# A twelve-stage network on one Trainium2 core: the decay chain of two state-space mixers cut into pieces, and a shared expert in three blocks

## The chip, the cores and the metric

The kernel is one program on one core of a Trainium2 chip. The core has engines that each run their own queue of instructions in order: TensorE (PE; loading weights is listed apart as PEld), VectorE (DVE), ScalarE (ACT), GpSimd (POOL) and SyncE (SP), which here only issues DMAs. They wait for one another through semaphores. The metric is the time of one execution on the device in microseconds (us), lower is better. Three executions of the kernel before took 2148.16, 2151.61 and 2161.24 us; the median is 2151.61 us.

## The reference

The network works on 1024 tokens in two sequences of 512, with 256 features in fp32. It has four layers, each of the form ffn, attention or mixer, ffn, and each part is added to the running `x`. The stages that the change touches are these:

```python
# layer 0, ffn (used twice): 32 experts, 6 per token, and one shared expert of width 352
x = x + 0.5 * _L0_ffn_ref(_layernorm(x, axis=-1), L0_ffn_wg_router, ...)
    sh = jax.nn.silu(x2d @ ws_gate) * (x2d @ ws_up) @ ws_down
    return y + sh
# layers 2 and 3, mixer: a gated state-space layer, 8 heads in layer 2, 64 in layer 3
    zxbcdt = u @ W_in                                  # u is the layer norm of x
    dt = jax.nn.softplus(dt + dt_bias)
    xBC = sum((xp[:, w:w + L, :] * conv_w[:, w] for w in range(D_CONV))) + conv_b
    xBC = jax.nn.silu(xBC)                             # split into x, B, C
    y, final_state = ssd(x * dt[..., None], A * dt, Bm, Cm, CHUNK)
    y = y + x * D_param[:, None]
    yf = y * jax.nn.silu(z)
    rrms = jax.lax.rsqrt(jnp.mean(yf * yf, axis=-1, keepdims=True) + 1e-05)
    y = yf * rrms * norm_w
    return y @ W_out
```

`dt` is a positive step size per token and head, `A * dt` its log decay (dA), and `ssd` sums over earlier tokens with weights exp(cumulative decay), within a chunk by a masked product and from chunk to chunk by a state.

## The kernel before

`x` stays in SBUF as 8 chunks of 128 tokens; a sequence of 512 tokens, 4 chunks, is called a row, 0 or 1 (the code's `b`). The stages run one after the other. Most of their order is chosen by a scheduler when the program is built; where `in_order` (L134) is used, the order in which the code is written is fixed on the engines named.

**Layer 0's shared expert.** `load_shared` (L266) loads gate, up and down weights and cuts the width of 352 into four blocks of 88. `shared_unit` (L280) does one row: for each block `front` (pg and pu at L291, silu at L294, product h at L295), and one block later `back`, which adds into `acc` (L301); at the end two adds into `x` (L319). Both rows run while `slot_lists` (L334) works out on DVE and PE in which slot each token of each expert goes (`sl_oh` L382, `ps_sl` L399, `ps_slt` L419, `sl_put` L428, `sl_get` L429). With `sl_get`, POOL starts to gather tokens (`xe`, L453); the experts then run on PE as units of `ps_xe` (transposes, L467), `ps_gu` (L477), `ps_he` (L491), `ps_ye` (L502), and POOL puts results back (`rows`, L507). The results are read back by `add_rows` (L621 to L628), which is put off until the next stage calls `settle` (L155).

**The mixers** (`mamba`, L1381 to L1806). One unit is a row and a group of 8 heads, one step is a chunk of 128 tokens of a unit. Layer 2 has one group, so 2 units and 8 steps; layer 3 has 8 groups, 16 units and 64 steps. Before the first step stands a prelude:

- `row(b)`: layer norm (DVE L181, L182, L193; POOL for the reciprocal root, L189 and L190), then 8 transposes (L169) into `xT`, half of it copied by DVE (L126), half by ACT (L128).
- `decay_sums(b)`: `pd` on PE (L1434), then a chain over DVE and ACT (softplus with Exp L1442 and Ln L1444, L1437 to L1451) to dA, then on PE `ps_row` (L1457), `ps_cum` (L1475) and two `ps_dec` (L1479). The cumulative rows `cr` go to DRAM (L1468, two DMAs for each group of heads) and come back broadcast to all partitions as `lm` and `ce` (L1581, L1584).
- `conv`: a projection `pp` (L1487), a scaled copy `cacc` on ACT (L1491), three taps on DVE (L1493), silu on ACT (L1496). It is used for B, C and the four pieces of x of a unit (`prep_front`, L1554); `prep_back` transposes a finished piece (`pt` L1567, copy `xt` L1568).
- `products` (L1515 to L1522): C times B. `exponents` (DVE, 8 instructions, L1594), `raised` (ACT exp, L1599) and `masked` (L1603) make the decay weights of two chunks.

In a step, PE computes the gate's input `pz` (L1618), the output `py` (L1646), the projection of the step before (L1691) and the new state `pst` (L1661); DVE adds to `y` (L1672) and POOL multiplies the gate in (L1673). A step also prepares one piece of the next unit. The steps are written in order for PE, ACT, DVE and POOL; the prelude isn't: the scheduler places it. Its program order is row 0's norm, `decay_sums(0)`, the convs of B and C and of unit 0, exponents and raised, then `row(1)` and `decay_sums(1)`, and then the steps. PSUM tiles of `psM` rotate through three buffers.

Of the kernel before, what the change touches and what calls it, by code (L numbers as in the profile page):

```python
# [79 lines left out]
class Net:  # L80
# [116 lines left out]
    def layernorm_T(self, es, psum):  # L197


        xT = es.enter_context(self.tc.tile_pool(name="xT", bufs=1)).tile([P, KD, T], F32, name="xT")  # L200
        p = es.enter_context(self.tc.tile_pool(name="ln", bufs=1))

        def row(b):
            xn = p.tile([P, CB, D], F32, tag="xn", name="xn")
            self.layernorm(p, xn, b)
            self.transpose_tokens(xn, xT, psum, b)

        return xT, row
# [57 lines left out]
    def load_shared(self, g, up, down, f, bw=88):  # L266
        nc = self.nc
        w = self.w("wsh")
        gv = w[:, : KD * f].rearrange("p (k f) -> p k f", k=KD)
        uv = w[:, KD * f : 2 * KD * f].rearrange("p (k f) -> p k f", k=KD)  # L270
        dv = w[:bw, 2 * KD * f : 2 * KD * f + f // bw * D].rearrange("p (c d) -> p c d", d=D)
        nc.sync.dma_start(gv, g.rearrange("(k p) f -> p k f", p=P))
        nc.sync.dma_start(uv, up.rearrange("(k p) f -> p k f", p=P))
        nc.sync.dma_start(dv, down.rearrange("(c p) d -> p c d", p=bw))
        return [
            (gv[:, :, i * bw : (i + 1) * bw], uv[:, :, i * bw : (i + 1) * bw], dv[:, i, :], bw)
            for i in range(f // bw)
        ]
# [728 lines left out]
    def l1_ffn(self):  # L1007
        nc, tc = self.nc, self.tc
        with ExitStack() as es:
            psM = es.enter_context(tc.tile_pool(name="f1m", bufs=8, space=PSUM))  # L1010
            xT, row = self.layernorm_T(es, psM)
# [286 lines left out]
    def l2_ffn(self):  # L1298
        nc, tc = self.nc, self.tc
        E = 8  # L1300
        with ExitStack() as es:
            psM = es.enter_context(tc.tile_pool(name="f2m", bufs=8, space=PSUM))
            xT, row = self.layernorm_T(es, psM)
# [77 lines left out]
    def mamba(self, pre, win, wout, nh):  # L1381
# [11 lines left out]
        TOP = 85.0  # L1393
        wname, win, wout = win, a[pre + win], a[pre + wout]
        with ExitStack() as es:
            psM = es.enter_context(tc.tile_pool(name=pre + "m", bufs=3, space=PSUM))
            xT, row = self.layernorm_T(es, psM)
# [22 lines left out]
            rows = dram.tile([2, NG, NC, HG * P], F32, name="rows")  # L1420
            wk = es.enter_context(tc.tile_pool(name=pre + "w", bufs=2))

            def decay_sums(b):
# [18 lines left out]
                nc.scalar.activation(t1, t2, AF.Exp)  # L1442
                nc.vector.tensor_scalar(t2, t1, 1.0, None, ALU.add)
                nc.scalar.activation(da, t2, AF.Ln)  # L1444
                nc.vector.scalar_tensor_tensor(t2, t2, -1.0, t1, ALU.add, ALU.subtract)
# [10 lines left out]
                for cc in range(CB):  # L1456
# [6 lines left out]
                    )  # L1463
                nc.vector.tensor_copy(cr[:, 0, :], ps)
                nc.scalar.activation(cr[:, 1, :], ps, AF.Exp)
                for g in range(NG):
                    for i in range(2):
                        nc.sync.dma_start(  # L1468
                            rows[i, g, bs].rearrange("c (h t) -> h c t", t=P),
                            cr[g * HG : (g + 1) * HG, i, :].rearrange("h (c t) -> h c t", t=P),  # L1470
                        )
# [4 lines left out]
                nc.vector.tensor_tensor(jb[:, bs, :], jb[:, bs, :], ps, ALU.subtract)  # L1476
                for out, lhsT in ((dec, self.c["gt"]), (cd, self.ones)):
# [5 lines left out]
            def conv(wv, m, b, out):  # L1483

                pp = psM.tile([P, S], F32, tag="mm", name="pp")
# [4 lines left out]
                acc = wk.tile([P, S], F32, tag="cacc", name="cacc")  # L1490
                nc.scalar.mul(acc, pp, cw[:, m, 3:4])  # L1491
                for w in range(2, -1, -1):
                    nc.vector.scalar_tensor_tensor(  # L1493
                        acc[:, 3 - w :], pp[:, : S - 3 + w], cw[:, m, w : w + 1], acc[:, 3 - w :], ALU.mult, ALU.add
                    )
                return lambda: nc.scalar.activation(out, acc, AF.Silu, bias=cb[:, m : m + 1])  # L1496
# [5 lines left out]
            def conv_b(b):  # L1502
                BTs[b] = wk.tile([P, S], F32, tag="BT", name="BT", bufs=1)
                conv(wb[:, :, 0:P], NX, b, BTs[b])()

            def conv_c(b):
                conv(wb[:, :, P : 2 * P], NX + 1, b, CT[:, b * S : (b + 1) * S])()
# [46 lines left out]
            def prep_front(u, m):  # L1554
                wo, g = u["wo"], u["g"]
                silu = conv(u["wx"][:, :, m * P : (m + 1) * P], g * NM + m, u["b"], u["xc"][:, m, :])
# [5 lines left out]
                return rest  # L1562
# [10 lines left out]
            def fetch(u, cc):  # L1573
# [7 lines left out]
                nc.sync.dma_start(k["lm"].rearrange("p h t -> p (h t)"), rows[0, u["g"], c].partition_broadcast(P))  # L1581
                if cc > 0:
                    k["ce"] = wk.tile([P, HG, P], F32, tag="ce", name="ce", bufs=3)
                    nc.sync.dma_start(  # L1584
                        k["ce"].rearrange("p h t -> p (h t)"), rows[1, u["g"], c].partition_broadcast(P)
# [150 lines left out]

            row(0)
            decay_sums(0)
            conv_b(0)
            conv_c(0)  # L1740
            for i in range(min(2, len(order))):
                fetch_wx(*order[i])
            unit(0)
            for i in range(3):
                chunk(i)
            products(0)
            for m in range(NM):
                prep_front(us[0], m)()
                if m:
                    prep_back(us[0], m - 1)  # L1750
            for i in (0, 1):
                exponents(ks[i])
            raised(ks[0])
            back = (us[0], NM - 1)
            row(1)
            decay_sums(1)


            tail = {}
            for s in range(NS):  # L1760
# [4 lines left out]
                with self.in_order(tail):  # L1765
# [9 lines left out]
                    rest = prep_front(unit(n + 1), cc) if nxt else None  # L1775
# [22 lines left out]
                with self.in_order(tail):  # L1798
                    new_state(k)

                    if last and cc == 0:
                        conv_b(1)
                    elif last and cc == 1:
                        conv_c(1)
                    elif last and cc == CB - 1:
                        products(1)  # L1806
            squares(ks[NS - 1])
# [66 lines left out]
```

## Time and profile before

| | us |
|---|---|
| median of three executions | 2151.61 |
| the profiled execution's own time | 2080.09 |
| its span, first to last instruction | 2078.0 |
| PE busy in it | 1786.1 |
| DVE, ACT, POOL busy | 1150.1, 791.6, 872.2 |
| layer 0's first ffn: first `pg` to first expert transpose `ps_xe` | 34.16 to 88.12 |
| the same in its second call, `ps_xe` | 518.72 |
| layer 2's mixer: first transpose to first `py` | 978.37 to 1036.69 |
| layer 3's mixer: first transpose to first `py` | 1324.76 to 1396.15 |

All lines of the profile come from one execution, so durations are compared with that execution's 2080.09 us. A timeline line gives start and duration in us, the engine, the line of code, the operation, output<-inputs, sizes and the number of instructions in the group; in brackets stands how long the engine was idle before it and what ended that. SPq is a DMA issue on SP. The granted clock is the share of TensorE's full clock that the chip allowed; over the whole span it was 0.912.

### The profile page before, as it was taken

How to read it: one execution, taken by the hardware profiler on the slowest of the kernel's cores; microseconds unless marked ns; L12 is line 12 of the kernel's file. 1: busy time of each engine (PE TensorE's matmuls, PEld its weight loads, DVE VectorE, ACT ScalarE, POOL GpSimd, SP SyncE). 2: the span in 40 equal slices, each digit the busy share in tenths (PEclk: the TensorE clock that was granted, in tenths of full speed). 3: DMA queues.
4: the chain of work that ended last, by engine and by line, in shares of the span. 5: the costliest groups of instructions: out<-in, count | busy, mean ns of one | idle time of the engine just before them, and what ended most of it. 6: DMA issues, size and time to landing. Idle time of an engine off the chain costs nothing. (4 is left out here: it accounts for less than half of the span.)

```text
span 2078.0 us, 29564 instructions
## 1 busy us (share of the span) xinstructions
PE 1786.1 (86%) x10590; PEld 1283.9 (62%) x10590; DVE 1150.1 (55%) x2725; ACT 791.6 (38%) x1336; POOL 872.2 (42%) x808
## 2 busy tenths in 40 slices
PE   5999859889999369889697989469999999999895
PEld 3677636565777247654476457347777677777664
DVE  4433266126333566556563653368777767777443
ACT  1132224210223024310562012357777667777211
POOL 3377646302777101000042026115666546676353
PEclk9999979989999669989797989679999999999798
DMA  8266450141565600000230013324444435444132
GB/s 294 62 194 187 144 187 2 31 143 34 177 183 154 221 0 1 21 1 0 93 103 21 11 36 98 106 98 153 155 153 159 153 121 174 153 163 134 42 94 94
DMA packets 117590, 226.03 MB, mean 109 GB/s; under 512 B 22532, under 2 KB 68978, under 8 KB 117292
## 3 DMA queue, kind: packets, MB, share of 16 engines
q1 hardware_dynamic: 88284, 170.17, 24.8%
q0 software_dynamic: 20608, 48.45, 7.3%
q10 hardware_dynamic: 8528, 5.26, 0.8%
q8 instruction: 93, 1.52, 0.3%
q14 instruction: 77, 0.63, 0.1%
HBM read 195.13 MB, written 41.81 MB: 114 GB/s over the span
## 5 line engine op out<-in xcount | busy, mean ns | idle before, releaser
L453 POOL DMA_INDIRECT xe<-table,sl_get x176 | 179.9, 1022 | 210.3 <-DVE sl_get L429 150.7
L477 PE MATMUL ps_gu<-we,xeT 128*128 128x352 f32 x704 | 228.3, 465 | 0.0
L507 POOL DMA_INDIRECT rows<-ye,sl_put x176 | 177.1, 1006 | 88.3 <-issue 41.4
L1493 DVE SCALAR_TENSOR_TENSOR cacc<-pp,L_attn_cols,cacc 128x511 f32<-128x511 f32 (+2 forms) x240 | 179.1, 748 | 55.5 <-ACT cacc L1491 50.2
L189 POOL TENSOR_SCALAR ln_rstd<-ln_mv 128x4 f32<-128x4 f32 x22 | 5.1, 233 | 420.1 <-DVE ln_mv L182 418.7
L502 PE MATMUL ps_ye<-we,hT 88*128 88x256 f32 x704 | 168.3, 379 | 2.9 <-ACT ye L128 1.6
L482 DVE SCALAR_TENSOR_TENSOR he<-se,xe,ps_gu 128x176 f32<-128x176 f32 x176 | 70.0, 398 | 174.3 <-ACT se L481 165.1
L477 PEld LDWEIGHTS ps_gu<-we,xeT 128*128 128x128 f32 x704 | 127.7, 193 | 54.7 <-issue 2.5
L502 PEld LDWEIGHTS ps_ye<-we,hT 88*128 88x128 f32 x704 | 133.0, 190 | 37.0 <-ACT ye L128 3.6
L1594 DVE SCALAR_TENSOR_TENSOR lm<-lm,jb,top 128x128 f32<-128x128 f32 x576 | 154.4, 343 | 0.0
L1618 PE MATMUL pz<-xT,wt 128*128 128x128 f32 x1152 | 143.1, 278 | 9.7 <-DVE cacc L1493 5.6
L1691 PE MATMUL yacc<-wt,y 128*128 128x256 f32 x576 | 145.8, 396 | 0.7 <-POOL y L1673 0.7
L1618 PEld LDWEIGHTS pz<-xT,wt 128*128 128x128 f32 x1152 | 136.2, 194 | 14.6 <-issue 9.2
L1487 PE MATMUL pp<-xT,wx 128*128 128x512 f32 x288 | 143.2, 623 | 0.3 <-ACT cd L1480 0.3
L1673 POOL TENSOR_TENSOR y<-y,sg 128x512 f32<-128x512 f32 x72 | 91.5, 1271 | 103.4 <-DVE y L1672 95.3
L1611 POOL TENSOR_TENSOR ce<-ce,CT 128x1024 f32<-128x1024 f32 x54 | 127.9, 2369 | 0.0
L169 PE MATMUL ps_tr<-cst,xn 128*128 128x128 f32 x176 | 42.5, 401 | 94.3 <-DVE xn L193 83.5
L1691 PEld LDWEIGHTS yacc<-wt,y 128*128 128x128 f32 x576 | 104.9, 192 | 25.4 <-issue 12.0
L1333 PE MATMUL ps_y<-w8T,xT 128*128 128x512 f32 x256 | 117.8, 614 | 0.0
L1646 PE MATMUL py<-lm,xt 128*64 128x128 f32 x1152 | 109.1, 284 | 5.9 <-issue 5.4
L481 ACT ACTIVATE se<-ps_gu 128x176 f32<-128x176 f32 x176 | 55.9, 318 | 149.8 <-PE ps_gu L477 149.7
L1603 DVE TENSOR_TENSOR lm<-lm,M 128x1024 f32<-128x1024 f32 x72 | 87.2, 1215 | 41.8 <-ACT lm L1599 40.3
(373 smaller groups left out, 3540.4 us busy)
## 6 DMA issues: line engine op xcount, KB each, us to landing
lm<-rows SPq DMA_DIRECT2D x72, 512.0 KB
ce<-rows SPq DMA_DIRECT2D x54, 512.0 KB
rows<-zero POOLq DMA_DIRECT2D x16, 768.0 KB, 10.0
y<-rows SPq DMA_DIRECT2D x16, 768.0 KB
we<-in_L_ffn_w_gate_dram SPq DMA_DIRECT2D x64, 176.0 KB
we<-in_L_ffn_w_up_dram SPq DMA_DIRECT2D x64, 176.0 KB
we<-in_L_ffn_w_down_dram SPq DMA_DIRECT2D x64, 176.0 KB
we<-in_L_ffn_w_dram SPq DMA_DIRECT2D x48, 176.0 KB
```

What stands on the lines that cost most here:

```text
L453: nc.gpsimd.indirect_dma_start(xe[:, i, :], None, table, bass.IndirectOffsetOnAxis(get[:, e * per + j : e * per + j + 1], 0), bounds_check ...
L477: nc.tensor.matmul(pg, xeT[:, k, i * P : (i + 1) * P], wgu[:, :, k], start=(k == 0), stop=(k == KD - 1))
L502: nc.tensor.matmul(py[:, i, :], hT[:, q, i * P : (i + 1) * P], wd[:, q, :], start=(q == 0), stop=(q == 1))
L507: put_rows = nc.gpsimd.indirect_dma_start(rows, bass.IndirectOffsetOnAxis(put[:, e * per + j : e * per + j + 1], 0), y[:, i, :], None, bou ...
L1333: nc.tensor.matmul(ps, xT[:, k, cs], self.w8T[:, k, 2 * e2 : 2 * e2 + 2, :], start=(k == 0), stop=(k == KD - 1))
L1487: nc.tensor.matmul(pp, wv[:, k, :], xT[:, k, b * S : (b + 1) * S], start=(k == 0), stop=(k == KD - 1))
L1493: nc.vector.scalar_tensor_tensor(acc[:, 3 - w :], pp[:, : S - 3 + w], cw[:, m, w : w + 1], acc[:, 3 - w :], ALU.mult, ALU.add)
L1594: nc.vector.scalar_tensor_tensor(k["lm"][:, h, :], k["lm"][:, h, :], jb[:, k["c"], n : n + 1], top, ALU.add, ALU.min)
L1611: nc.gpsimd.tensor_tensor(k["ce"], k["ce"], ct, ALU.mult)
L1618: nc.tensor.matmul(pz[:, m, :], u["wz"][:, kk, m * P : (m + 1) * P], xT[:, kk, c * P : (c + 1) * P], start=(kk == 0), stop=(kk == KD - 1),)
L1646: nc.tensor.matmul(py[i * HP : (i + 1) * HP, m, :], w[:, h * HP : (h + 1) * HP], v[:, h, :], start=(m == 0 and n == 0), stop=(n == len(src ...
L1691: nc.tensor.matmul(yacc[cc // 2][:, cc % 2, :], k["y"][:, m, :], u["wo"][:, m, :], start=(u["g"] == 0 and m == 0 and cc % 2 == 0), stop=(u ...
```

## The change

Three things are changed. First, the shared expert's blocks are as wide as the 128 partitions where more than two are needed: 352 is cut into 128, 128 and 96, and the down weights come in two DMAs. A width of 176 stays at two blocks of 88.

Second, `decay_sums` becomes a generator that stops at four places (behind the Exp, behind the Ln, behind `ps_row`, behind `ps_cum`), so that its pieces can be placed between other work, and `conv` returns its taps and its silu apart. `row` is split into `norm` and `turn`. The whole prelude stands in one order written out by hand for PE, ACT and DVE. In layer 2 (`few`), row 1's norm and turn follow row 0's first piece, and its decay chain is placed among the convs of unit 0. In layer 3, row 1's results of the expert stage are added to `x` ahead of C's taps (`settle(1)`), and its norm, turn and chain are hung on steps 0 to 4 (`later`), at the end of each.

Third, the DRAM layout of the rows has no group index any more, so that two DMAs per row of tokens write it, in place of two per group. The buffers of `cacc` are three in layer 3.

```diff
-    def load_shared(self, g, up, down, f, bw=88):
+    def load_shared(self, g, up, down, f):
+        n = -(-f // P)
+        bw = P if n > 2 else f // n
...
-        nc.sync.dma_start(dv, down.rearrange("(c p) d -> p c d", p=bw))
+        full = f // bw
+        nc.sync.dma_start(dv[:bw, :full], down[: full * bw].rearrange("(c p) d -> p c d", p=bw))
+        if full < n:
+            nc.sync.dma_start(dv[: f - full * bw, full], down[full * bw :])
...
-            rows = dram.tile([2, NG, NC, HG * P], F32, name="rows")
+            rows = dram.tile([2, NC, nh * P], F32, name="rows")
...
                 nc.scalar.activation(t1, t2, AF.Exp)
+                yield
                 nc.vector.tensor_scalar(t2, t1, 1.0, None, ALU.add)
                 nc.scalar.activation(da, t2, AF.Ln)
+                yield
...
+                yield
                 nc.vector.tensor_copy(cr[:, 0, :], ps)
                 nc.scalar.activation(cr[:, 1, :], ps, AF.Exp)
-                for g in range(NG):
-                    for i in range(2):
...
+                for i in range(2):
+                    nc.sync.dma_start(
+                        rows[i, bs].rearrange("c (h t) -> h c t", t=P),
+                        cr[:, i, :].rearrange("h (c t) -> h c t", t=P),
+                    )
...
                 nc.vector.tensor_tensor(jb[:, bs, :], jb[:, bs, :], ps, ALU.subtract)
+                yield
...
-                acc = wk.tile([P, S], F32, tag="cacc", name="cacc")
+                acc = wk.tile([P, S], F32, tag="cacc", name="cacc", bufs=2 if few else 3)
...
-            row(0)
-            decay_sums(0)
-            conv_b(0)
-            conv_c(0)
...
-            row(1)
-            decay_sums(1)
+            later = {}
             tail = {}
+            with self.in_order(tail, ("PE", "Activation", "DVE")):
+                row(0)
+                fetch_wx(*order[0])
+                d0, d1 = decay_sums(0), decay_sums(1)
+                next(d0)
+                if few:
+                    row(1)
+                bt, bs_ = conv_b(0)
+                bt()
+                next(d0)
+                ct, cs_ = conv_c(0)
+                self.settle(1)
+                ct()
+                next(d0)
+                if few:
+                    bs_()
+                    cs_()
+                unit(0)
+                fetch_wx(*order[1])
+                pf = [prep_front(us[0], 0)]
+                pf[0][0]()
+                next(d0)
+                next(d0, None)
+                if few:
+                    next(d1)
+                    next(d1)
+                else:
+                    bs_()
+                    cs_()
+                for i in range(3):
+                    chunk(i)
+                pf.append(prep_front(us[0], 1))
+                products(0)
+                pf[1][0]()
+                pf[0][1]()
+                pf[1][1]()
+                prep_back(us[0], 0)
+                pf.append(prep_front(us[0], 2))
+                pf[2][0]()
+                pf[2][1]()
+                prep_back(us[0], 1)
+                if few:
+                    next(d1)
+                    next(d1)
+                    next(d1, None)
+                exponents(ks[0])
+                exponents(ks[1])
+                pf.append(prep_front(us[0], 3))
+                pf[3][0]()
+                pf[3][1]()
+                raised(ks[0])
+                prep_back(us[0], 2)
+                back = (us[0], NM - 1)
+                if not few:
+                    later[0] = [lambda: norm(1)]
+                    later[1] = [lambda: turn(1), lambda: next(d1)]
+                    later[2] = [lambda: next(d1), lambda: next(d1)]
+                    later[3] = [lambda: next(d1)]
+                    later[4] = [lambda: next(d1, None)]
...
                     new_state(k)
...
+                    both(later.get(s, ()))
```

## Prediction, made before the result was known

> **What bounds the kernel now.** I read the page's head and busy shares first, then busy time by stage, then the order of time on TensorE (PE) at the three places that the diff touches.
>
> ```profile
> span 2078.0 us, 29564 instructions
> PE 1786.1 (86%) x10590; PEld 1283.9 (62%) x10590; DVE 1150.1 (55%) x2725; ACT 791.6 (38%) x1336; POOL 872.2 (42%) x808
> ```
>
> PE is busy for 86%, so an edit pays where it shortens PE's work or opens one of PE's gaps. By stage (window; its length; busy us and instructions of PE, weight load, DVE, ACT, POOL; granted TensorE clock; DMA share; GB/s):
>
> ```profile
> 34.00:74.00 40.00, 37.42 (x378) 20.88 (x378) 31.54 (x121) 5.30 (x8) 1.78 (x4) 1.00 0.24 78
> 74.00:88.00 14.00, 13.11 (x45) 7.65 (x43) 3.52 (x7) 1.19 (x2) 10.49 (x11) 1.00 0.28 77
> 978.00:1000.00 22.00, 13.07 (x51) 7.93 (x52) 11.03 (x34) 9.21 (x16) 1.26 (x2) 0.77 0.40 136
> 1000.00:1020.00 20.00, 13.59 (x42) 7.19 (x42) 13.52 (x25) 13.25 (x18) 0.00 (x0) 0.83 0.24 89
> 1020.00:1036.00 16.00, 11.37 (x53) 7.63 (x53) 3.72 (x14) 8.35 (x15) 0.21 (x1) 0.68 0.01 2
> 1376.00:1396.00 20.00, 14.57 (x61) 11.58 (x60) 7.00 (x16) 7.71 (x13) 0.72 (x1) 0.58 0.06 14
> 1396.00:1440.00 44.00, 44.00 (x334) 33.56 (x334) 35.32 (x79) 34.45 (x49) 27.66 (x20) 1.00 0.40 134
> ```
>
> Layer 0's shared expert (34 to 88) fills PE at full clock. The preludes of layer 2's mixer (978 to 1037) and layer 3's (1325 to 1396) leave PE idle for a quarter to two fifths, at a clock of 0.58 to 0.83: chains set their length, not work. Layer 3's steps (from 1396) leave PE no gap at all, with DVE and ACT at 80%.
>
> **Part 1, the shared expert in 3 blocks.** The hand-over to the experts, PE and POOL:
>
> ```profile
> 64.76 4.37 PE L399 MATMUL ps_sl<-sl_ol,sl_oh 128*32 128x64 f32 x224 [1.90 <-DVE sl_oh L382]
> 83.49 3.62 PE L301 MATMUL acc<-wsh,h 88*128 88x256 f32 x16
> 88.12 0.71 PE L467 MATMUL ps_xe<-cst,xe 128*128 128x128 f32 x4 [1.01 <-DMA xe<-table,sl_get]
> ...
> 74.47 1.11 POOL L453 DMA_INDIRECT xe<-table,sl_get  x1 [36.84 <-DVE sl_get L429]
> 75.88 1.03 POOL L453 DMA_INDIRECT xe<-table,sl_get  x1 [0.30 <-issue]
> ```
>
> A block of one half costs 4 matmuls for pg, 4 for pu and 8 for acc: three groups of 1.72 us (PE starts them at 78.33, 80.06, 81.77 and 83.49), 5.16 us. The matmuls' row count doesn't change with a block of 128 in place of 88. One block less, two halves, two calls: 4 x 5.16 = 20.6 us of PE work leave. Not all of it is time. The routing chain on DVE (sl_oh, until PE's 64.76) isn't shortened, and the same PE work lies ahead of it in both orders. So the saving falls behind it: PE, at 70.5 when ps_sl ends, has three acc groups left (5.2 us, and the turn of the slot table), not two fronts and five acc groups, and is through at about 77. Then the gathers set the start. They come at 1.30 us each from 74.47; elsewhere (gather at 1237.32 for 1.16, its ps_xe at 1240.54) a gather is used 2.1 us after its end. The first ps_gu needs two units, four gathers: 78.52 + 1.00 + 2.1 + 0.6 for ps_xe = 82.2. It stood at 90.22: **-8.0**. In the second call the fourth gather (509.21) comes some 0.7 later, behind one x add of L319: 513.6 for 520.82, **-7.2**. Bounds: -9 each if gathers land sooner, -4 each if POOL takes it back. The second load of `down` and the smaller ACT and DVE count lie under PE's work: nothing. Sum -15.2 (-8 to -18).
>
> **Part 2, layer 2's prelude.** Now, PE in order of time:
>
> ```profile
> 1026.67 1.87 PE L1457 MATMUL ps_row<-cst,dA 128*8 128x128 f32 x8 [3.40 <-DVE dt L1451]
> 1030.73 3.78 PE L1487 MATMUL pp<-xT,wx 128*128 128x512 f32 x4 [0.29 <-ACT cd L1480]
> 1036.69 1.09 PE L1646 MATMUL py<-lm,xt 128*64 128x128 f32 x16
> 1038.68 1.88 PE L1487 MATMUL pp<-xT,wb 128*128 128x512 f32 x4
> ```
>
> Row 1's chain stands alone from 1020.5 to 1030.7: 10.2 us that the change opens. What it adds is a fixed order on PE, ACT and DVE, in place of the scheduler's, which today runs exponents on DVE at 998 to 1004 while it waits. I add up along the new order. Row 1's norm (4 x 0.41, 1.47 waiting for POOL's rstd, 1.4) and turn end at 989.4; before, conv B started at 989.50, so it costs nothing yet. Conv B at half clock 3.2, its cacc 0.69, taps 2.3 (1015.32: six in 4.54): 995.6. Conv C's taps end at 999.1, and only behind them stand row 0's four dA instructions, so ps_row is at 1000.0 (it was at 985.43). Conv x0 stands behind ps_row on PE: its taps run 1006.1 to 1008.4 (now 1005.23). Behind them: cr, jb, ps_dec, row 1's pd (2.0), its Exp, Ln and two table loads of 1.28, the products; x1's taps end at about 1018 to 1020 (13.4 now). ACT then runs both silus and pt's copies ahead of x2's cacc: x2's taps end at 1026.5 to 1028 (about 1017.6). Row 1's dA, ps_row (1.9), cr: 1032. Both exponents, 16 x 0.27 = 4.3: 1036.7. x3's taps 2.3, silu with its load 2.0, raised with its load 3.2, 1043; masked 1.2, pz and py: 1047.1. It was 1036.69: **+10.4**, and the steps behind keep their order. The opened 10.2 us is overspent because exponents, taps and silus, which ran beside the convs, are now one behind the other.
>
> The size hangs on TensorE's clock. The row first: pp x4 takes 3.78 us at 1030.73 and 1.88 at 1038.68. The Trainium skill (TensorE: Matmul & The Clock Gate, Part 1: The HAM clock gate) has half rate after an idle window of about 3.4 us, and full rate only after as much sustained work. My chain leaves PE no 3.4 us of work at a stretch, so by the rule nearly every record on it runs cold: +10 to +12. By the rows of this prelude (granted 0.68 to 0.83) it would be warm for half of the time: about +7. All warm, seven groups at 1 us or so less: +3; all cold with an unlucky phase: +13. I take +10.4: the convs, pd and ps_row on the path are those that follow a gap.
>
> **Part 3, layer 3.** Now:
>
> ```profile
> 1375.40 2.19 PE L169 MATMUL ps_tr<-cst,xn 128*128 128x128 f32 x8 [9.67 <-DVE xn L193]
> 1377.73 3.78 PE L1434 MATMUL pd<-wb,xT 128*128 128x64 f32 x16
> 1386.80 1.94 PE L1457 MATMUL ps_row<-cst,dA 128*64 128x128 f32 x8 [5.28 <-DVE dA L1448]
> 1391.39 2.61 PE L1487 MATMUL pp<-xT,wx 128*128 128x512 f32 x4
> 1396.15 1.09 PE L1646 MATMUL py<-lm,xt 128*64 128x128 f32 x16
> ```
>
> From the x adds at 1367.97 to 1391.4, 23 us, row 1 is on the path of the first py. Moved to the steps, it leaves. The same sum along the new order: x adds (8, 2.8 us) now ahead of C's taps, dA to 1342, ps_row and x0's conv to 1346, cr 1350, B and C's silus 1353 to 1355, x1's taps to 1360, x2's 1367, exponents to 1371, x3's taps 1373, raised 1377, py 1381: **-15** (-12 to -16 with the clock's phase). The sixteen row DMAs (5.74 us of issue on SP) become two; nothing waits for them: exponents came 16 us after cr and come 16 us after it again. Row 1's four y loads (2.1 us of issue on SP) move from 1346.97 to about 1317, behind the first wx load; row 0's were used 2.5 us after issue, these have 17: nothing, and C's taps would wait as long as they were late. The second wx load and wt, 2.1 us later, are needed 20 us on.
>
> The steps then pay. PE's work is only 5.4 us: 8 transposes 1.1, pd 1.9, row, sums and decays 2.4 at full clock. But it comes with waits in the middle of full queues:
> - Step 0: DVE holds row 1's norm, and xn waits for POOL's rstd, behind the y gate (1.27) on POOL; exponents, taps and raised of step 1 stand behind xn.
> - Step 1: ACT's half of the xT copy stands behind raised (1.91 and its 1.28 load). pd waits for it, runs cold after that gap (3.8), and DVE waits for pd with masked(2) behind it. Against the pitch of 8.2 to 9.0 this step takes 19.6: +11.
> - Step 2: ps_row stands ahead of the next pp on PE and waits for DVE's t2, ACT's Ln with a load, four DVE instructions of 0.46: step 16.6 for 8.6, +8.
> - Steps 3 and 4: under 1 each. On SP row 1's two stores wait for cr, and the lm loads issued behind them are for three steps ahead: nothing; without that lead, one step of 8.6.
> Sum +20. Lower end: PE's work alone, +5.4, if the queues have that much slack; DVE and ACT, at 80% of a 44 us stretch, leave 9 us each, and 8.7 us of DVE work (norm, copy, chain) and 5.8 of ACT come in. Less than 5.4 is excluded, as PE has no gap in these steps. Upper end +23 with the clock cold in steps 1 and 2. I take +20, as both waits stand in the order itself. Layer 3: **+5** (-10 to +11).
>
> **The sum.** -15.2 + 10.4 + 5 = +0.2 us on the profiled execution's 2080.09 (span 2078.0). The runs' median, 2151.61, is 1.034 times that, so 2151.8.
>
> **Rivals.**
> - *The overlap works as drawn* (0.15). Against me: waits of 1.5 us for POOL are short, and a few extra instructions could slip in beside work. Layer 3 then gains 15 - 5.4 = 10, layer 2 about 3 (10.2 opened, 7 spent), the shared expert 15: -28, x 1.034: 2123. Against it: ps_row ahead of pp in step 2, which no slack of another engine hides.
> - *The clock falls in layer 3's steps* (0.12), slower. Place: steps 1 to 4. These run at clock 1.00 only because PE has no gap; waits of 11 and 8 us open one. Price: half of about 40 us of PE work at half rate, +20 beside my +20, and +13 in layer 2: -15 + 13 - 15 + 40 = +23, x 1.034: 2175. It decides once the steps lose more than 20 us in all, and is over 1% from about 39. Against it: conv, pz and the projection refill PE for over 6 us right after each wait.
> - *POOL takes the shared expert's gain* (0.10). In the experts gathers and puts fill POOL at 5.31 us per unit (xe at 101.92, 107.23, 112.54), PE's pace is 5.0. If the lead of the gathers is used up, the earlier start is given back: -2 in place of -15, +13: 2165. Against it: gathers start when they did and lead by three units, so a drift of 0.3 per unit isn't used up in 32 units.
> - *My sum* (0.63), 2138 to 2164 by itself.
>
> One per cent, 21.5 us, is about what can be told from no change here (the three runs span 13 us). From these cases: faster by more 0.13, within 0.74, slower by more 0.13. The range 2128 to 2170 leaves out most of the first two rivals and holds the rest.
>
> **What would show it.** In the new profile: the first ps_gu at about 82 in place of 90.22 and an equal shift in the second call; the time from layer 2's first ps_tr to its first py 69 us (58.3 now) with conv clocks near 0.5; in layer 3 that stretch 56 to 57 us (71.4 now), and the third and fourth py 17 to 20 us after the ones before (8.6 now), with PE waiting for dA at ps_row and DVE for pd. I am wrong if those steps keep their pitch, if layer 2's convs run warm, or if the experts' pace in layer 0 slows from 5.0 to 5.3.

## The result and the profile after

The changed kernel takes 2182.19 us (median of four, 2181.16 to 2182.57) against 2149.89 us of the kernel before (2146.0 to 2161.24) in the same set of runs: a ratio of 1.0141, 95% interval 1.0102 to 1.018, 32 us slower. The forecast was 2151.8 with a range to 2170.

The kernel before takes about 2150 us in some sets of runs and about 2079 us in others, with the same code; the runs of one set share a chip, and times are compared only within a set. They are called 2150 sets and 2079 sets below. The profile before (2080.09 us) is from a 2079 set, the first times and the profile after (2181.16 us) from a 2150 set. The factor of 1.034 in the prediction, taken for a ratio of timed to profiled runs, is this difference. In a 2079 set (e5 below) the changed kernel takes 2101.53 against 2078.18: 1.0111 (1.0089 to 1.0133), 23 us slower. In both sets the loss is above the 18 us that the range allowed.

The page's head and busy shares, changed kernel:

```profile
span 2179.2 us, 29393 instructions
PE 1812.6 (83%) x10526; PEld 1295.1 (59%) x10526; DVE 1150.0 (53%) x2721; ACT 787.9 (36%) x1335; POOL 872.5 (40%) x808
```

DVE, ACT and POOL do as much as before to within 4 us. PE has 64 instructions fewer, as a block of the shared expert is gone in two rows and two calls. It is busy 26 us longer than in the profile before, at a granted clock of 0.898 for 0.912, but these two profiles are from sets of different kinds. Between profiles of 2079 sets PE's busy time is the same, 1788.3 us in e5 and 1788.8 in e1 (the kernel before), at 0.900 and 0.909: the change costs waiting, not busy time.

Layer 2's prelude on PE in order of time (start, us, engine, line, operation; in brackets the idle time before and what ended it), from the first transpose at 1028.68 on:

```profile
1048.79 1.87 PE L1472 MATMUL ps_row<-cst,dA 128*8 128x128 f32 x8 [5.55 <-DVE dt L1466]
1050.59 3.68 PE L1504 MATMUL pp<-xT,wx 128*128 128x512 f32 x4
...
1058.66 3.59 PE L1447 MATMUL pd<-wb,xT 128*128 128x8 f32 x16
1062.09 3.76 PE L1504 MATMUL pp<-xT,wx 128*128 128x512 f32 x4
...
1080.53 1.13 PE L1472 MATMUL ps_row<-cst,dA 128*8 128x128 f32 x8 [3.14 <-DVE dt L1466]
...
1097.46 3.78 PE L1639 MATMUL pz<-xT,wt 128*128 128x128 f32 x16 [3.04 <-ACT xt L1588]
1101.16 1.39 PE L1667 MATMUL py<-lm,xt 128*64 128x128 f32 x16
```

The first py comes 72.5 us behind the first transpose, 58.3 before. The four convs of x take 3.54 to 3.76 us for four matmuls, at a granted clock of 0.50 to 0.55, where 1.88 is the time at full clock; B and C, just ahead of them, take 4.34 for eight at 0.83.

Layer 3's steps 1 to 4 on the same engine:

```profile
1483.91 1.11 PE L169 MATMUL ps_tr<-cst,xn 128*128 128x128 f32 x4 [3.96 <-DVE cacc L1512]
1485.70 0.69 PE L1447 MATMUL pd<-wb,xT 128*128 128x64 f32 x2 [0.68 <-DVE xT L126]
1488.41 3.25 PE L1447 MATMUL pd<-wb,xT 128*128 128x64 f32 x14 [2.03 <-ACT xT L128]
...
1505.08 1.97 PE L1472 MATMUL ps_row<-cst,dA 128*64 128x128 f32 x8 [3.34 <-DVE dA L1463]
1506.98 3.78 PE L1504 MATMUL pp<-xT,wx 128*128 128x512 f32 x4
...
1530.16 1.98 PE L1504 MATMUL pp<-xT,wx 128*128 128x512 f32 x4 [3.00 <-ACT state L1684]
```

And what DVE and ACT do in front of pd (DVE's scaling of row 1, its wait for pd; ACT's raised and the copy behind it), and, last, what ACT waits for ahead of the state copy that releases pp in step 4:

```profile
1474.70 4.86 DVE L193 TENSOR_SCALAR xn<-x,ln_mv,ln_rstd 128x256 f32<-128x256 f32 x4 [1.47 <-POOL ln_rstd L190]
...
1491.70 0.42 DVE L1450 TENSOR_TENSOR dt<-pd,L_attn_prm 128x256 f32<-128x256 f32 x1 [6.06 <-PE pd L1447]
...
1485.98 1.91 ACT L1620 ACTIVATE lm<-lm 128x2048 f32<-128x2048 f32 x1
1487.80 0.57 ACT L128 COPY xT<-ps_tr 128x512 f32<-128x512 f32 x1
...
1528.52 0.51 ACT L1579 ACTIVATE wt<-wt,L_attn_cols 128x256 f32<-128x256 f32 x1 [4.52 <-DMA wt<-n_L_attn_out_proj_w_dram]
```

Where the time went, between two executions in 2079 sets, e1 (the kernel before, span 2078.6) and e5 (the changed kernel, span 2102.5), by the first transpose of each stage and the first py:

| stretch | before | after | difference |
|---|---|---|---|
| layer 0: start to the stage behind its second ffn | 708.5 | 696.5 | -12.0 |
| from there to layer 2's mixer | 271.1 | 272.1 | +1.0 |
| layer 2's mixer (first py behind first transpose) | 140.5 (58.3) | 155.5 (72.5) | +15.0 |
| layer 2's second ffn and layer 3's first | 205.8 | 210.8 | +5.0 |
| layer 3: first transpose to first py | 71.5 | 59.7 | -11.8 |
| layer 3: first py to the last ffn | 550.6 | 576.5 | +25.9 |
| the last ffn | 130.7 | 131.4 | +0.7 |
| sum | 2078.6 | 2102.5 | +23.9 |

The pitch from py to py at the start of layer 3 is 6.99, 24.4, 15.97, 8.19, 12.67 us in e5; in e1 it is 6.02, 8.61, 8.63, 7.76, 7.81.

### The profile page after: what moved, and what is told of

It reads as the page before. It is cut to its first block, busy times and chain, and to the rows that moved or that the text cites. A ratio compares the mean times of both kernels' runs of the same rounds, so it can differ in the third digit from the quotient of the medians.

```text
span 2179.2 us, 29393 instructions
## 1 busy us (share of the span) xinstructions
PE 1812.6 (83%) x10526; PEld 1295.1 (59%) x10526; DVE 1150.0 (53%) x2721; ACT 787.9 (36%) x1335; POOL 872.5 (40%) x808
## 5 line engine op out<-in xcount | busy, mean ns | idle before, releaser
L489 PE MATMUL ps_gu<-we,xeT 128*128 128x352 f32 x704 | 240.8, 485 | 0.0
L514 PE MATMUL ps_ye<-we,hT 88*128 88x256 f32 x704 | 177.3, 394 | 39.1 <-DVE hT L126 15.4
L489 PEld LDWEIGHTS ps_gu<-we,xeT 128*128 128x128 f32 x704 | 135.1, 204 | 60.3 <-issue 12.0
L1639 PE MATMUL pz<-xT,wt 128*128 128x128 f32 x1152 | 146.4, 282 | 16.0 <-ACT xt L1588 10.4
L1639 PEld LDWEIGHTS pz<-xT,wt 128*128 128x128 f32 x1152 | 139.1, 197 | 21.6 <-ACT xt L1588 11.8
L1504 PE MATMUL pp<-xT,wx 128*128 128x512 f32 x288 | 148.4, 641 | 4.0 <-ACT state L1684 3.0
L128 ACT COPY xT<-ps_tr 128x512 f32<-128x512 f32 x22 | 12.9, 584 | 296.0 <-PE ps_tr L169 279.2
```

The source lines that it names most:

```text
L489: nc.tensor.matmul(pg, xeT[:, k, i * P : (i + 1) * P], wgu[:, :, k], start=(k == 0), stop=(k == KD - 1))
L514: nc.tensor.matmul(py[:, i, :], hT[:, q, i * P : (i + 1) * P], wd[:, q, :], start=(q == 0), stop=(q == 1))
L1504: nc.tensor.matmul(pp, wv[:, k, :], xT[:, k, b * S : (b + 1) * S], start=(k == 0), stop=(k == KD - 1))
L1639: nc.tensor.matmul(pz[:, m, :], u["wz"][:, kk, m * P : (m + 1) * P], xT[:, kk, c * P : (c + 1) * P], start=(kk == 0), stop=(kk == KD - 1),)
```

## The experiments

The theory was the prediction's: three parts with a sum near nothing. When the result was known, the first trace also showed the experts of layer 0 slow, in stages whose code is the same. That made two rivals: the change provokes the slow experts, or they belong to the set of runs. The runs e1 to e4 are one set, e5 to e8 another, e9 to e11 a third and e12 to e15 a fourth; all but the third are 2079 sets. What the expectations of e2 to e4 say in absolute times starts from 2150.

**e1, the kernel before once more.**

> The kernel before, unchanged, for a profile from the chip that also runs the three kernels beside it. The changed kernel's trace loses time in stages that the change does not touch: from the first expert transpose of layer 0 to the next stage 395.2 us in the first call (362.9 in the profile before) and 226.6 in the second (188.1), and 98.5 for 84.2 in layer 3's first ffn. Theory A (the pace of the experts is not the change's doing; the profile before was a lucky execution): this profile shows the same long expert stages, 390 to 400 and 220 to 230 us, at a span near 2150. Theory B (the change provokes it, by an earlier start of the experts or by the place of the code): here the units again come every 5.0 us, 363 and 188 us, at a span near 2080.

Measured: 2079.78 (2072.44 to 2082.16) at a ratio of 1.0004, units at 5.0 us. This alone doesn't decide, since the kernel before takes 2079 in the whole set; e5 does.

**e2, only the shared expert in 3 blocks.** The head of the edit:

```diff
-    def load_shared(self, g, up, down, f, bw=88):
+    def load_shared(self, g, up, down, f):
...
+        n = -(-f // P)
+        bw = P if n > 2 else f // n
...
```

> Only the shared expert in 3 blocks. By the landmarks of the two traces (34 to 88 us became 32 to 76, 464 to 519 became 485 to 530) it should give -21 us if the experts run at their own pace: 2129 (theory A). If the earlier start provokes slow experts (theory B), the gain is given back and more: 2150 to 2165.

Measured: 2059.73, ratio 0.9908 (0.9891 to 0.9924), 19 us faster. PE at the hand-over to the experts:

```profile
71.83 4.16 PE L305 MATMUL acc<-wsh,h 128*128 128x256 f32 x18
76.97 0.36 PE L471 MATMUL ps_xe<-cst,xe 128*128 128x128 f32 x1 [0.98 <-DVE x L323]
78.53 0.75 PE L471 MATMUL ps_xe<-cst,xe 128*128 128x128 f32 x3 [1.20 <-DMA xe<-table,sl_get]
80.91 1.18 PE L471 MATMUL ps_xe<-cst,xe 128*128 128x128 f32 x4 [1.63 <-DMA xe<-table,sl_get]
81.88 2.56 PE L481 MATMUL ps_gu<-we,xeT 128*128 128x352 f32 x4
```

The shared work ends at 76, the first transposes then wait twice for gathers, and the first ps_gu starts at 81.9. The last unit is transposed at 231.1 (239.3 in e1), 8.2 earlier. The gathers are the limit that the prediction named. Of the 20 us between the profiles of e1 and e2, 12.8 lie in layer 0. Another 8.6 lie in layer 3, whose code is the same; there ACT's wait for weights is 19.1 us in place of 26.0 (see e12). That part isn't the shared expert's own work, and e5, with a wait of 25.9 us, doesn't have it.

**e3, only the mixers**, the shared expert in 4 blocks of 88.

> Only the two mixers' change, the shared expert in its old 4 blocks. By the landmarks: layer 2 +15 (first transpose to the next stage's 155.5 for 140.5), layer 3 +7.5 (631.5 for 624.0): 2150 + 22 = 2172 (theory A). By theory B, if the shared expert's blocks are to blame for the slow experts, the same +22; if any change of code does it, more, 2180 or above.

Measured: 2116.85, ratio 1.0178 (1.0159 to 1.0197), 38 us slower, 16 more than expected. Against e1, layer 2's mixer is the expected 15.0 longer; the two ffns behind it are 5.5 longer, and layer 3's mixer is 19.0 longer in place of 7.5. ACT's wait for weights is 30.0 us in it, 26.0 in e1. e2 and e3 add up to +19, e5 measured +23.

**e4, only layer 2's prelude**; layer 3's prelude as before, with two row DMAs for each row and three buffers of `cacc`.

> Only layer 2's prelude as changed; layer 3 keeps its old order (with the two row DMAs in place of sixteen). By the landmark +15 us: 2165. First transpose to first py 72 us in place of 58, PE at half clock in most of it. If the row-1 chain in the open were worth moving, -5.

Measured: 2104.87, ratio 1.0117 (1.0092 to 1.0141), 26 us slower, 11 more than expected. The mixer itself is 15.0 longer. Another 5 come behind it, in layer 3's first ffn, whose code is the same: its 32 router matmuls take 6.83 us here and in every other kernel with a new layer 2 prelude, 3.78 to 3.95 in the kernels with the old one. The rest lies in layer 3, 8.4 longer than in e1 with an old prelude: its steps of row 0 lose 8.6 (the prelude and row 1 nearly cancel), and ACT's wait for weights, which e12 takes up, is 31.4 us for 26.0. Over all runs with layer 3's old prelude and old order of loads its mixer takes 613 us (e2, wait 19.1) to 630 (e4, wait 31.4), so a difference of some us there isn't a part's own cost. The difference of e3 and e4, 38 - 26 = +12 for layer 3, has this uncertainty.

**e5, the changed kernel again.**

> The changed kernel again, on a chip on which the kernel before and the kernel with 3 blocks keep the experts' units at 5.0 us. If the parts add up and the slow experts of the first trace belong to that chip or execution, not to the change: 2079 - 19 + 38 = 2098 us, ratio 1.009, with units at 5.0 us. If the combination of the parts provokes the slow experts, they are slow here too: 2140 to 2180.

Measured: 2101.53, ratio 1.0111 (1.0089 to 1.0133), experts' units at 5.0 us. So the change doesn't provoke slow experts, and the parts add up to within some 4 us. The other side is shown by e9 and e10: in their 2150 set the experts are slow with the shared expert in its old 4 blocks. Whether the chip or the moment makes such a set, no run separates.

**e6, layer 2 alone, the fixed order kept, row 1's chain put back to the end.**

```diff
-                if few:
-                    row(1)
                 bt, bs_ = conv_b(0)
...
                 back = (us[0], NM - 1)
+                if few:
+                    row(1)
+                    for _ in d1:
+                        pass
```

> Layer 2 alone, with the prelude still in one fixed order on PE, ACT and DVE, but row 1's norm, turn and decay chain back behind everything else, where the kernel before has them. Theory H (the fixed order is what costs, since exponents, convs and silus no longer run beside each other): still 15 us or more over the kernel before. Theory C (row 1's pieces, waiting in front of the convs' instructions, are what costs): first py 58 to 60 us behind the first transpose, time within 4 us of the kernel before. My own working has both, with 10 us of chain at the end and some 5 to 8 of lost overlap: +6.

Measured: 2091.73, ratio 1.0069 (1.0048 to 1.009), 13.5 us slower: 8.4 in the mixer, 5.0 in the two ffns behind it. The first py comes 67.8 us behind the first transpose: 9.5 of the 14.2 us are this fixed order, 4.7 the place of row 1's pieces in it.

**e7, layer 2 alone, the changed program order, nothing fixed.**

```diff
-            with self.in_order(tail, ("PE", "Activation", "DVE")):
+            with (nullcontext() if few else self.in_order(tail, ("PE", "Activation", "DVE"))):
```

> Layer 2 alone, the changed program order, but the prelude left to the scheduler as in the kernel before (nothing fixed on PE, ACT and DVE). Theory H: within 4 us of the kernel before or up to 8 under it, as row 1's chain may fill the gaps. Theory C: the +26 of the changed order stay for the most part.

Measured: 2078.73, ratio 1.0005 (0.9993 to 1.0016). PE in that prelude, first transpose at 979.48:

```profile
989.21 1.04 PE L1468 MATMUL ps_row<-cst,dA 128*8 128x128 f32 x8
990.43 1.96 PE L1500 MATMUL pp<-xT,wx 128*128 128x512 f32 x4 [0.19 <-issue]
...
1035.23 1.21 PE L1663 MATMUL py<-lm,xt 128*64 128x128 f32 x16
```

The first py comes after 55.8 us, 2.5 sooner than before; the ffns behind, with the router at 6.83, take back more than that. Theory H holds for layer 2: the same instructions, in the program order of the change, cost nothing when the scheduler may place them. As e7 also has the two row DMAs and the third buffer, these cost nothing either.

**e8, layer 3 alone, one hop between engines for each step.** The scaling is split from the statistics, ps_row from the chain in front of it.

```diff
-                    later[0] = [lambda: norm(1)]
-                    later[1] = [lambda: turn(1), lambda: next(d1)]
-                    later[2] = [lambda: next(d1), lambda: next(d1)]
-                    later[3] = [lambda: next(d1)]
-                    later[4] = [lambda: next(d1, None)]
+                    later[0] = [lambda: norm.stats(1)]
+                    later[1] = [lambda: norm.scale(1)]
+                    later[2] = [lambda: turn(1)]
+                    later[4] = [lambda: next(d1)]
+                    later[5] = [lambda: next(d1)]
+                    later[6] = [lambda: next(d1)]
+                    later[7] = [lambda: next(d1), lambda: next(d1)]
+                    later[8] = [lambda: next(d1, None)]
```

> Layer 3 alone, with row 1's pieces in steps 0 to 8 at one hop between engines for each step: the statistics in step 0, the scaling in 1, the turn in 2, pd and Exp in 4, Ln in 5, dA in 6, ps_row and cr in 7, the last sums in 8. Layer 3's change as made costs +12 here (mixers less layer 2: 2116.9 - 2104.9), with 15.2, 8.6 and 4.1 us lost in steps 1, 2 and 4. If the waits in the full queues are the loss, and not the work: the steps lose 8 or less in all, and with the prelude's -13 this kernel is 5 to 9 us under the kernel before (2070 to 2074). If the added work itself is the loss, it stays at +10 or more.

Measured: 2082.8, ratio 1.0029 (1.0019 to 1.0038), 4.6 slower: between the two expectations. The prelude gains 13.3. The first nine steps still lose 14 in all (7.14, 11.95, 12.06, 7.76, 9.54, 8.62, 10.1, 11.18, 8.69), where e3 and e5 lose 28 and 29. So about half of the loss was waits in the wrong place, and the other half stays in this spread.

**e9, layer 3 alone, the change's pieces on even steps.**

```diff
-                    later[1] = [lambda: turn(1), lambda: next(d1)]
-                    later[2] = [lambda: next(d1), lambda: next(d1)]
-                    later[3] = [lambda: next(d1)]
-                    later[4] = [lambda: next(d1, None)]
+                    later[2] = [lambda: turn(1), lambda: next(d1)]
+                    later[4] = [lambda: next(d1), lambda: next(d1)]
+                    later[6] = [lambda: next(d1)]
+                    later[8] = [lambda: next(d1, None)]
```

> Layer 3 alone, row 1's pieces as in the change, each with the same instructions, but hung on steps 0, 2, 4, 6 and 8 in place of 0, 1, 2, 3 and 4. Even steps have no raised on ACT in front of the turn's copy, and the turn stands a step behind the norm. If the copy behind raised and the norm just before it make step 1's loss of 15, that step falls to about +6, the dA step keeps its 8, the rest 4: steps +18, prelude -12, so +6 over the kernel before, half of the change's +12 to +16. If any place of pd and its chain costs the same, the steps stay at +26 and the kernel at +12 to +16.

Measured, in a set where the kernel before takes 2149.48: 2171.11, ratio 1.0096 (1.0079 to 1.0113), 21.6 us slower. This expectation failed. The steps are 7.12, 15.88, 13.16, 7.76, 19.41, 9.71, 9.73, 7.76, 15.31. With the norm alone in step 0, the next step still loses 7.3, as the expectation had it (+6), and turn and pd, free of raised, lose 4.5. So about half of step 1's 15.8 is the norm; of the other 8.5, some 4 went with the new place. But the chain of dA loses 11.6 in its new place, where ACT also waits 2.84 us for weights ahead of the Ln, and the whole is no better.

**e10, layer 3 alone, row 1's chain in the prelude as in layer 2, order left to the scheduler, nothing on the steps.**

```diff
-            with self.in_order(tail, ("PE", "Activation", "DVE")):
+            with nullcontext():
...
-                if few:
+                if True:
                     row(1)
```

> Layer 3 alone: row 1's norm, turn and chain stay in the prelude, among the convs as the change has it in layer 2, nothing hangs on the steps, and the prelude's order is left to the scheduler. In layer 2 this took the first py from 58.3 to 55.8 us behind the first transpose. If the same holds here, the first py comes some 60 to 68 us behind the first transpose (71.5 before), the steps keep their pitch, and the kernel is 4 to 11 us under the one before. If row 1's x adds and chain delay row 0's convs as much as they save: no difference.

Measured, same set as e9: 2149.08, ratio 1.0003 (0.9986 to 1.002). The first py comes 59.9 us behind the first transpose, as hoped, the steps keep their pitch, and yet nothing is gained: from there to the last ffn it takes 559.0 us, 549.8 in e11 of the same set, whose layer 3 prelude is the old one. In both, layer 3 takes 619.0 in all. ACT's wait for weights is 31.3 us here and 23.6 in e11.

**e11, 3 blocks and layer 2 left to the scheduler.**

> The shared expert in 3 blocks together with layer 2's new program order left to the scheduler; layer 3 as before. The parts add up to -19 and 0: 2059, 20 us under the kernel before and the fastest so far, or 2 us under the 3 blocks alone if layer 2's -2 of stage time shows.

Measured, same set as e9 and e10: 2146.26, ratio 0.9976 (0.9957 to 0.9994), 3 us faster, not 20. In this set the experts' units take 5 to 12 us. With 4 blocks (e10) they run from 87.6 to 263.4 and the next stage's first transpose is at 474.9; with 3 blocks (e11) they run from 75.9 to 263.4, next stage at 475.5. The earlier start is worth nothing there. The gathers aren't late: from the eighth unit on they end some 20 us ahead of their use in e10 and e11. What the trace of such a set shows is engines that stand still with their input ready; in e10 PE is done with a `ps_he` at 155.7 and DVE, idle since 155.5, starts its copy at 158.15. For part of these waits the profile finds no instruction that ended them and calls them remote. One entry of ACT in the profile after (us in total, times, longest):

```profile
ACT se L493 <- remote: 33.7, 15, 3.8
```

Over all engines such waits come to 55 to 62 us in each of the four profiles from 2150 sets, and to none in the thirteen from 2079 sets. What causes them, no run here shows.

**e12, the kernel before with the wt loads first.** In e10 and in the kernel before, ACT's scaling of the next unit's output weights waits for their DMA, which stands on SP behind lm and ce loads that wait for a free buffer.

```diff
                         fetch_wx(*order[n + 2])
+                    if cc == 0 and nxt:
+                        unit(n + 1)
                     chunk(s + 3)
```

> The kernel before, with one change: in the first step of a unit the load of the next unit's wt is issued ahead of the lm and ce loads, which wait on SP for a free buffer. ACT waits for wt 25 to 31 us in all, seven times in row 0, and the first steps of those units take 9.1 to 9.6 us for 7.75 in row 1. If these waits set the steps: 1.5 us for each of 6 units and up to 5 at the turn of the rows, 9 to 14 us under the kernel before. If they are covered: no difference.

Measured: 2068.09, ratio 0.9947 (0.9927 to 0.9966), 10.7 us faster. ACT's waits for that DMA in e1 and in e12, one line from each:

```profile
ACT wt L1559 <- DMA wt<-n_L_attn_out_proj_w_dram: 26.0, 7, 4.3
```

```profile
ACT wt L1559 <- DMA wt<-n_L_attn_out_proj_w_dram: 1.9, 4, 0.6
```

Layer 3 from first py to the last ffn falls from 550.6 to 539.5.

**e13, e10 with the wt loads first.**

> e10 (layer 3's row 1 in the prelude among the convs, order left to the scheduler) with the wt loads first. If e10's 11 us were given back in the wait for wt: 11 us under e12, 20 to 25 under the kernel before. If they went elsewhere: as e12.

Measured: 2053.55, ratio 0.9878 (0.9858 to 0.9899), 25 us faster. First py after 57.8, the rest 539.6, as in e12: now the 13.7 us of the shorter prelude are kept. ACT's wait for weights is 3.1 us; in e10 the gain had gone into it.

**e14, 3 blocks again.**

> The shared expert in 3 blocks alone once more. On a chip where the kernel before takes about 2079 us: -19. On one where it takes about 2150 us, and the experts' units come every 5 to 10 us in place of 5.0: the experts of the first call end where they ended before (about 263 us), and the kernel gains 4 us or less.

Measured: 2060.66, ratio 0.9907 (0.9883 to 0.993), where the kernel before takes 2078.79; as e2.

**e15, 3 blocks and e13's layer 3, layer 2 as before.**

> 3 blocks, layer 3 as in e13, layer 2 as before. If the parts add up: e13's gain and e14's: 40 us under the kernel before where the experts run at 5.0 us, 20 to 25 where they don't.

Measured: 2042.72, ratio 0.9826 (0.9806 to 0.9846), 36 us faster than the kernel before and, by the ratios of e15 and e5, 2.8% faster than the changed kernel. The gains of e13 and e14 would add up to 43. Layer 0 gives its 12.9 us here as in e2; what is missing is e2's and e14's gain in layer 3, the shorter wait for weights, which e13 has already removed. So 3 blocks by themselves are worth 12 to 13 us, not 19. It was run only in a set with units at 5.0 us.

## Why the prediction was wrong

The forecast was no change, and the kernel is 1.4% slower: the time lies 12 us above the range. The places were the ones forecast, and in layers 2 and 3 the mechanisms too. Four terms of the sum failed: the shared expert's gain did not last in the first set, the losses of layers 2 and 3 were too small, and a stage outside the change was put at nothing.

- *Shared expert, -15.2.* The start came as forecast in both sets: the first ps_gu at 81.9 in e2 and 81.1 in the profile after (forecast 82.2). Where the experts run at 5.0 us the gain lasts: the end of the first call's units moved by -7.9 in e5 (forecast -8.0), the second call's share by another -7.2 up to its next stage's start (forecast -7.2). Between the first call's last unit and the next stage 3.2 us were lost, so -12.0 stayed; that stretch takes 209.8 us in e1 and 212.9 in the profile before, of the same kernel, so the 3.2 aren't shown to be the change's. In the 2150 sets the gain is gone: e10 against e11, with no other difference up to there, shows starts 11.7 us apart and the same end. The step that failed there is that an earlier start is kept through the experts. This is the outcome of the rival with POOL (the experts take the gain), not its mechanism: POOL's gathers and puts keep their 1.0 us each and the gathers stay about 20 us ahead, and it is ACT and DVE that stand still. Why they do stays open. With it, -15 becomes about 0.
- *Layer 2, +10.4.* The chain was right in kind, and e6 and e7 bear it out. The prelude measured +14.2, 1 above the upper bound. Both exponents were done 60.7 us behind the first transpose, forecast 58.3. From there the working has a slip: 1036.7 with 2.3, 2.0 and 3.2 is 1044.2, not 1043. These two are 3.6 of the 3.8 us. On the clock, the rule that the prediction takes from the Trainium skill (TensorE: Matmul & The Clock Gate, Part 1: The HAM clock gate), half rate after an idle window, would in the prediction's reading have nearly every record on the path cold. The trace agrees for the four convs of x, at 0.50 to 0.55, and not for B and C, at 0.83; the mean over the prelude was 0.70, 0.77 before. pz, which the working took at full clock, waited 3.04 us for ACT's copy and took 3.78.
- *Outside the change, 0 in the sum.* The ffns between the two mixers took 5 us more with no change of code, +3.05 of it in 32 router matmuls that fell into half clock. No term for it was in the working.
- *Layer 3, -15 + 20.* The prelude gave -11.8 (e5) to -13.3 (e8). In e5 the steps lost 1.0 (step 0), 15.8 (step 1, forecast 11), 7.3 (step 2, forecast 8), 0.4 and 4.9 (steps 3 and 4, forecast under 1 each): 29 for 20. Both waits of the working are there, pd's for ACT's copy and ps_row's for dA. In step 1 two rows were mis-sized: the norm's scaling, 1.38 us for four in the preludes and 4.86 in the step, and pp behind pd, 3.73 in place of 1.88. In step 4 the two ps_dec take two of the three `psM` buffers, so pp waits for the state copy (2.13 us in e5, 3.00 in the profile after), and this stands on ACT behind the wait for the output weights, 3.65 us in e5 and 1.86 in the same step of e1: the wait of e12. Over the whole of layer 3 it is +14.2 in e5 for +5.
- *The rival of the clock* (0.12) came in part. Over steps 0 to 4 the granted clock is 0.83 in e5 and 1.00 in e1. By the rows of pp, pt and pz against their times at full clock this is worth about 5 us, an estimate, where the rival had 20.
- *The scale of 1.034* was no scale. It added nothing to the forecast difference, as the sum was near 0, but it hid that the profile came from another kind of set than the times.

With the measured terms the sum is -12 + 1 + 15 + 5 + 14.2 + 0.7 = +24 where the experts keep their pace (e5: +23). For the first set there is no trace of the kernel before; its stages can be read from e10 (old code up to layer 3) and e11 (old layer 3). Against these the profile after has -3.6 in layer 0 (+0.5 against e9), +14.9 in layer 2's mixer, +7.1 in the ffns between, +12.4 in layer 3 and -1.0 in the last ffn: +30, near the +32 measured.

## What to carry to other kernels

A fixed order pays only where it beats what the scheduler finds. Here the program order of the change, left free in layer 2, lost nothing (e7), while the same order fixed made the mixer 17 us longer (e4, 155.5 for 138.6). Work taken off a serial stretch and hung on a loop whose bound engine has no gap cost far more than its own length here, 29 us of steps for what the prediction counted as 5.4 of PE's work, as each hop between engines became a wait at the head of a queue. Leaving it in the stretch, beside the work there, and then looking for the wait that takes the place of the one removed (here a weight load queued behind buffer waits) was worth 25 us (e13). And before a sum is made from one profile, its own time should be near the times that it is to forecast.

## What the runs showed of the hardware

Four DVE scalings of 128x256 take 1.38 us in a prelude and 4.86 us in a step, where POOL runs fp32 tensor_tensor work of 1.05, 2.40 and 1.09 us at the same time. The first line is a prelude's, from the profile after; the others, DVE and POOL, are from the changed kernel in e5:

```profile
1036.34 1.38 DVE L193 TENSOR_SCALAR xn<-x,ln_mv,ln_rstd 128x256 f32<-128x256 f32 x4 [1.47 <-POOL ln_rstd L190]
...
1403.03 4.86 DVE L193 TENSOR_SCALAR xn<-x,ln_mv,ln_rstd 128x256 f32<-128x256 f32 x4 [1.47 <-POOL ln_rstd L190]
...
1402.96 1.05 POOL L1655 TENSOR_TENSOR xd<-xt,dec 128x512 f32<-128x512 f32 x1
1403.96 2.40 POOL L1632 TENSOR_TENSOR ce<-ce,CT 128x1024 f32<-128x1024 f32 x1
1406.33 1.09 POOL L1676 TENSOR_TENSOR state<-state,cd 128x512 f32<-128x512 f32 x1
```

One by one, the four in the step take 1.13, 2.44, 1.13 and 0.40 us. The first three each end 0.15 us behind one of POOL's three instructions, and the fourth, behind all of these, is as short as one in a prelude (0.41). The Trainium skill (GPSIMD Engine Reference, 1. Specifications) says that POOL's interfaces to SBUF are shared with DVE and that DVE instructions in a 2-port perf mode or with two SBUF inputs contend for them. The rows agree with that, in five kernels (4.47 to 4.86 beside POOL, 1.38 without); which mode the scaling runs in no run shows, and none took POOL's work away to prove it. Other DVE instructions of a step keep their time beside POOL: one exponent takes 0.34 us and one tap 0.75 with POOL busy or idle. Each of these has one of its inputs in PSUM.

The granted clock alone moved 3.05 us in a stage that nothing had touched. The 32 router matmuls ran at a granted clock of 0.95 in e1 and of 0.50 in e5:

```profile
1209.41 3.78 PE L247 MATMUL ps_lg<-routerT,xT 128*128 128x8 f32 x32
...
1214.43 6.83 PE L255 MATMUL ps_lg<-routerT,xT 128*128 128x8 f32 x32
```
